# Preparing the two graphs of a pair side by side, with the edge test on VectorE and the counts of other entries on ScalarE

## The chip, the cores and the metric

The kernel runs on one core of one Trainium2 chip. The metric is the device time of one execution in microseconds (us). The core has five engines that run at the same time and each take their instructions in order: PE (TensorE, the matrix unit), DVE (VectorE), ACT (ScalarE), POOL (GpSimd) and SP (SyncE, which here only issues transfers). ACT and POOL issue transfers as well. An instruction that waits holds up everything behind it on its own engine.

## The reference

There are 16 graphs of 1024 nodes with 64 channels, given as `x` (16, 1024, 64), a symmetric float32 adjacency of zeros and ones `adj` (16, 1024, 1024) and a node mask. Each layer works on `h = relu(layernorm(x))`.

```
# layer 0, per graph
neigh = (adj > 0) & ~eye                     # the neighbours of each node
rank  = cumsum(neigh) - neigh;  nb = neigh.sum(-1)
skip  = ceil(nb / 2) if nb > 10 else 1
rem   = neigh & (skip > 1) & (rank % skip == skip - 1) & mask ;  rem |= rem.T
nd    = (neigh & ~rem) | eye                 # what stays: the "live" neighbours
agg   = .25*q25 + .5*q50 + .25*q75           # quantiles over live neighbours, per channel
x = x + MLP(h + agg) * mask
# layer 1: three graph convolutions  x_i = bn(relu(adj @ (x_{i-1} @ W_i) + b_i)), then a linear layer
```

## The kernel before

**Two stages.** The first stage finds the live neighbours and the quantiles for 8 pairs of graphs, one pair after another; the second (`later`) runs the dense part of both layers and is woven into the end of the first.

**Within a pair.** Preparing a pair (`prepare`) reads the adjacency in 8 tiles of 128 rows for each graph and ends with a table `r` that numbers every node's live neighbours. Nodes are sorted by their number of live neighbours and cut into eight blocks (`BLOCKS` and `TAIL`) of 200 to 16 columns. For each block `gather` builds selection masks on DVE (tile `s`, L987), multiplies them with the features on PE (tile `pg`, L1018; the two graphs fill the two halves of the partitions), and copies the sums out on ACT (tile `g`, L1023). `quantiles` then sorts the slots of the block with a network of min and max on DVE (L935), weighted with coefficients from ACT (L868, L871), and multiplied and added on DVE (L941, L950). The block that is sorted and the block that is gathered are one apart. Seven of the block steps of a pair also carry a share of the next pair's preparation.

**The preparation of one graph** (`prepare_one`, then `find_live` and `number_slots`, which it returns). For each of 8 row tiles: a 512 KB load into tile `a` (two buffers, L664, issued by SP), ACT makes `edge` by the sign (L671), DVE counts entries that are neither 0 nor 1 into `odd` (L673), PE transposes (`ptE`, L678), ACT copies the result into `edgeT` (L681). SP then sends `edgeT` to memory (L684) for the second stage, and DVE clears its diagonal (`own`, L686), so it waits for that transfer. Then come the row sums (`sums`, L651), the running counts (`cs` on PE, `stays` on ACT and DVE, L725 and L726), the live edges with their number `nv` (`q` on PE, L752 on ACT), and the place of each node in the order by degree: `key` (L758), eight comparisons on ACT (L770), `place` (L773). POOL sends the rows to memory by place (L778, eight indirect transfers) and fetches them again in order (`lp`, L794, two buffers); PE and ACT transpose them into `liveT` (L809, L812); sums, `nvs` (L822) and a test against `bounds` (L829, L833) follow; `number_slots` writes `r` in two sides of eight copies each (L851). `prepare` ends with the weights `z` (L615 to L618) and the three bf16 parts `hp` of the features (L625 to L628). Only when `r` side 0, `z` and `hp` of both graphs are there can the next pair's first block be gathered.

**What sets the order.** Everything is written as generators whose `yield`s are steps. `weave` draws them by share of the sort done; `SHARES` says how many preparation steps each block carries, 93 in a pair. Before, the two graphs follow each other: all of `prepare_one` for graph 0 and then for graph 1, then `find_live` and side 0 of `number_slots` for each. Side 1 of both is kept for the next pair's first steps. From this order a planner makes the final order of every engine's queue at build time: it may let an instruction pass earlier ones on its engine, but on the chip each queue then runs strictly in order. Buffers by name: `a` has two, `byte` (for `edge`, `edgeT`, `liveT`) four, `stays` one, the PSUM tile `big` two, `coef` one.

**The rest that the change touches.** `bounds` is a constant tile filled on POOL at the start (L472 to L492). At the end a flag is formed from `odd` and `beyond` (L1496 to L1509); if it is set, a general path runs, which this data never needs.

Of the kernel before, what the change touches and what calls it, by code (L numbers as in the profile page):

```python
# [10 lines left out]
F32 = mybir.dt.float32  # L11
# [19 lines left out]
SHARES = (10, 9, 17, 24, 20, 13, 0)  # L31
# [368 lines left out]

@with_exitstack
def graph_layers_kernel(ctx: ExitStack, tc: tile.TileContext, ins, out: bass.AP):
# [61 lines left out]
    bounds = const.tile([C, HALF], BF16, name="bounds")  # L464
# [7 lines left out]
    with tc.tile_pool(name="setup", bufs=2) as setup:  # L472
        for c in range(1, NT + 1):
            most, least = [(-float(N), 0, N)], [(0.0, 0, N)]
            for (j0, j1, few, slots), (first, end, fewer) in zip(BLOCKS + (TAIL,), NEAR):
                if c == NT:
                    least.append((float(few), j0, j1))
                    most.append((-float(slots), j0, j1))
                    for k in sorted(fewer, reverse=True):
                        most.append((-float(k), j0, j0 + fewer[k]))  # L480
                if c in first:
                    most.append((-float(first[c]), j0, j1))
                if c in end:
                    least.append((float(end[c]), j0, j1))
            for row, pieces in ((c - 1, most), (NT + c - 1, least)):
                line = setup.tile([1, N], BF16, tag="line", name="line")
                for value, a, b in pieces:
                    nc.gpsimd.memset(line[:, a:b], value)
                for hf in range(NH):
                    nc.gpsimd.dma_start(  # L490
                        out=bounds[32 * hf + row : 32 * hf + row + 1, :], in_=line[:, hf * HALF : (hf + 1) * HALF]
                    )  # L492

    odd = const.tile([P, NB, NT], F32, name="odd")
# [74 lines left out]

    h_d = [dram.tile([N, C], F32, name=f"h_d{b}") for b in range(NB)]  # L570
# [14 lines left out]
    def prepare(p, pools):  # L585


        work, keep, ps = pools
        st = Pair()
        st.p = p  # L590
# [14 lines left out]
        find_live, number_slots = [], []  # L605
        for x in range(2):
            find_live.append((yield from prepare_one(st, x, pools)))
        for x in range(2):
            number_slots.append((yield from find_live[x]()))
            yield from number_slots[x](0)  # L610
# [19 lines left out]
        st.number = itertools.chain(*(number_slots[x](1) for x in range(2)))  # L630
# [23 lines left out]
    def prepare_one(st, x, pools):  # L654
# [14 lines left out]
        for t in range(NT):  # L669
            a, coming = coming, load(t + 1) if t + 1 < NT else None  # L670
            nc.scalar.activation(edge[:, t, :], a, AF.Sign, saturate=False)  # L671
            junk = work.tile([P, N], F8, tag="junk_v", name="junk_v")
            nc.vector.scalar_tensor_tensor(  # L673
                junk, a, 1.0, a, ALU.is_equal, ALU.not_equal, accum_out=odd[:, b, t : t + 1], saturate=False
            )
            pt = ps.tile([P, NT, P], F32, tag="big", bufs=2, name="ptE")
            for u in range(NT):
                nc.tensor.matmul(  # L678
                    out=pt[:, u, :], lhsT=edge[:, t, u * P : (u + 1) * P], rhs=ident_h, start=True, stop=True
                )  # L680
            nc.scalar.activation(edgeT[:, :, t * P : (t + 1) * P], pt, AF.Copy, saturate=False)  # L681
            yield
# [105 lines left out]
        def find_live():  # L788
# [36 lines left out]
            for hf in range(NH):  # L825
                sl = slice(hf * HALF, (hf + 1) * HALF)
                rows = slice(32 * hf, 32 * hf + 2 * NT)
                nc.tensor.matmul(out=by[:, sl], lhsT=chunk_to, rhs=sums[:, sl], start=True, stop=False)
                nc.tensor.matmul(  # L829
                    out=by[:, sl], lhsT=ident_h[rows, rows], rhs=bounds[rows, :], start=False, stop=True  # L830
                )
# [588 lines left out]
    with ExitStack() as stack:  # L1420
# [7 lines left out]
        with ExitStack() as inner:  # L1428
# [3 lines left out]
            )  # L1432
            ahead = Steps(prepare(0, early))
# [60 lines left out]
    with ExitStack() as stack:  # L1494
        ps = stack.enter_context(tc.tile_pool(name="ps_flag", bufs=1, space=PSUM))
        most_odd = const.tile([P, 1], F32, name="most_odd")  # L1496
        nc.vector.tensor_reduce(most_odd, odd.rearrange("p b t -> p (b t)"), AX.X, ALU.max)
        worst = const.tile([P, 1], F32, name="worst")
        nc.vector.tensor_copy(worst, most_odd)
        most_beyond = const.tile([2 * NT, 1], F32, name="most_beyond")  # L1500
        nc.vector.tensor_reduce(most_beyond, beyond, AX.X, ALU.max)
        nc.vector.tensor_tensor(worst[: 2 * NT], worst[: 2 * NT], most_beyond, ALU.max)
        pd = ps.tile([1, P], F32, name="pd")
        nc.tensor.transpose(pd, worst, ident)
        most = const.tile([1, 1], F32, name="most")
        nc.vector.tensor_reduce(most, pd, AX.X, ALU.max)
        nc.vector.tensor_scalar(most, most, 0.0, None, ALU.is_gt)
        flag = const.tile([1, 1], I32, name="flag")
        nc.vector.tensor_copy(flag, most)  # L1509
# [28 lines left out]
```

## Time and profile before

| what | value |
|---|---|
| median of 3 runs (lowest, highest) | 3160.63 us (3157.54, 3173.24) |
| the profiled execution | 3163.56 us, of it span 3161.8 us |
| PE busy | 2599.2 us (82% of the span) |
| DVE busy | 2559.8 us (81%) |
| ACT busy | 1696.2 us (54%) |
| POOL busy | 619.5 us (20%) |
| mean granted clock of PE | 0.915 |
| until the first mask `s` of the first pair | 205.8 us |
| from the first mask of one pair to that of the next | 299.4, 300.1, 300.2, 293.0, 351.5, 294.1, 300.4 us |
| from the last pair's first mask to the end | 817 us |

The busy times are averages over stages of different kinds, so they are read by stage. The fifth interval between pairs is longer because the tails of four pairs are sorted in it. The times of first masks are starts of the first 128x3200 instruction of L987 in each pair, taken from the order of instructions in time (205.80, 505.23, 805.29, 1105.45, 1398.46, 1749.98, 2044.03, 2344.39 us).

### The profile page before, as it was taken

To read this page: it belongs to the slowest core of one execution; us is meant where nothing else is said; L and a number is where in the kernel's file an instruction comes from. 1 tells how busy PE (TensorE), PEld (TensorE's weight loads), DVE (VectorE), ACT (ScalarE), POOL (GpSimd) and SP (SyncE) were. 2 spreads that over 40 slices of the span, in tenths; PEclk is the share of its full clock that TensorE was granted. 3 is DMA by queue.
4 is the path that set the end of the run, shared out by engine and by line. 5 is a ranking of instruction groups with operands and counts; after the bars stand their busy time and mean duration, and the time that the engine had idled before them with its cause. 6 is when DMAs were issued, how large, how long until landed. Compare 5 with 4: busy or idle time off the path is not lost.

```text
span 3161.8 us, 67201 instructions
## 1 busy us (share of the span) xinstructions
PE 2599.2 (82%) x27849; PEld 1697.4 (54%) x27849; DVE 2559.8 (81%) x5895; ACT 1696.2 (54%) x3292; POOL 619.5 (20%) x545
## 2 busy tenths in 40 slices
PE   2678978898888889885798889888986688977778
PEld 1445655565556556653565566456643456644445
DVE  4149889998999799989998999899976979963332
ACT  4764666567557755774367557745853223332221
POOL 5110161022102200330022103300422530311110
PEclk9779999999899999997899999999987799988989
DMA  4131022111211212122111211211113011122211
GB/s 138 46 104 60 3 67 70 56 55 52 66 57 54 64 56 68 46 72 47 42 64 51 66 56 57 67 56 63 48 36 75 9 41 26 49 55 54 54 54 42
DMA packets 221082, 177.45 MB, mean 56 GB/s; under 512 B 189024, under 2 KB 189152, under 8 KB 216672
## 3 DMA queue, kind: packets, MB, share of 16 engines
q1 hardware_dynamic: 141824, 125.88, 13.1%
q0 software_dynamic: 17408, 37.81, 3.9%
q10 hardware_dynamic: 61536, 9.39, 1.7%
q8 instruction: 219, 3.59, 0.5%
q14 instruction: 95, 0.78, 0.1%
HBM read 124.44 MB, written 48.55 MB: 55 GB/s over the span
## 4 chain that ended last, share of the span: by engine, by line
DVE 40%; PE 29%; ACT 12%; DMA 8%; issue 6%; another core or an unknown queue 2%; POOL 2%; ACTq 1%; DVEq 0%; POOLq 0%; SPq 0%
PE pg L1018 11%; DVE t L935 10%; DVE s L987 9%; DVE g L935 8%; PE pg L1200 5%; ACT junk L770 3%; DMA a<-in_adj 3%; DMA lp<-live_d 3%; DVE junk_v L673 2%; PE pr L845 2%; DVE g_tails L935 1%; DVE t_tails L935 1%; PE keys L763 1%; PE pf L1216 1%
## 5 line engine op out<-in xcount | busy, mean ns | idle before, releaser
L1018 PE MATMUL pg<-s,hp 128*64 128x400 bf16 (+11 forms) x16848 | 1366.5, 313 | 172.3 <-DVE s L987 138.1
L1018 PEld LDWEIGHTS <-hp 128*64 128x64 bf16 x16848 | 894.5, 112 | 553.9 <-issue 109.6
L987 DVE TENSOR_SCALAR s<-r 128x3200 bf16<-128x3200 bf16 (+25 forms) x1312 | 623.6, 521 | 103.6 <-PE pg L1018 74.9
L778 POOL DMA_INDIRECT live_d<-edge,place x128 | 261.1, 2040 | 1354.3 <-DVE place L773 1149.9
L1023 ACT COPY g<-pg 128x400 f32<-128x400 f32 (+10 forms) x384 | 169.0, 443 | 399.4 <-PE pg L1018 363.1
L935 DVE TENSOR_TENSOR t<-g 128x600 f32<-128x600 f32 (+9 forms) x524 | 315.5, 626 | 34.0 <-ACT g L1023 33.2
L1200 PE MATMUL pg<-adjT,xw 128*64 128x512 fp8e4 x2304 | 284.5, 398 | 52.8 <-ACT xw L1185 25.7
L935 DVE TENSOR_TENSOR g<-t 128x96 f32<-128x96 f32 (+16 forms) x555 | 283.2, 537 | 1.2
L1243 POOL DMA_INDIRECT agg<-agg_d,place x128 | 171.2, 1338 | 495.2 <-PE pt L1131 258.2
L671 ACT ACTIVATE edge<-a 128x1024 fp8e4<-128x1024 f32 x128 | 135.1, 1058 | 214.4 <-DMA a<-in_adj 213.9
L1200 PEld LDWEIGHTS <-xw 128*64 128x64 bf16 x2304 | 140.1, 114 | 182.4 <-issue 42.0
L868 ACT ACTIVATE coef<-z,bias 128x200 f32<-128x200 bf16 (+6 forms) x480 | 173.9, 405 | 102.3 <-DVE agg L950 66.0
L935 DVE TENSOR_TENSOR t<-t 128x192 f32<-128x192 f32 (+20 forms) x447 | 207.8, 475 | 0.2
L871 ACT ACTIVATE coef<-coef,wcol 128x200 f32<-128x200 f32 (+7 forms) x512 | 189.6, 403 | 9.3 <-issue 7.1
L673 DVE SCALAR_TENSOR_TENSOR junk_v<-a 128x1024 fp8e4<-128x1024 f32 x128 | 155.4, 1214 | 24.4 <-DMA a<-in_adj 24.4
L845 PE MATMUL pr<-liveT,upto 128*128 128x512 fp8e4 (+2 forms) x384 | 127.4, 350 | 53.1 <-ACT r L851 46.9
L770 ACT ACTIVATE junk<-keys,minus 128x1024 fp8e4<-128x1024 f32 x128 | 144.3, 1128 | 38.1 <-PE keys L763 34.3
L851 ACT CAST r<-pr 128x592 bf16<-128x592 f32 (+1 forms) x256 | 142.5, 585 | 41.1 <-PE pr L847 32.1
L794 POOL DMA_DIRECT2D lp<-live_d x128 | 89.4, 699 | 376.9 <-PE pt L809 319.3
L812 ACT ACTIVATE liveT<-pt 128x1024 fp8e4<-128x1024 f32 x128 | 130.3, 1034 | 50.5 <-PE pt L809 47.1
L752 ACT ACTIVATE edge<-q,bias 128x1024 fp8e4<-128x1024 f32 x128 | 141.8, 1108 | 22.6 <-PE q L747 22.6
L725 ACT ACTIVATE stays<-cs,back 128x1024 f16<-128x1024 f32 x128 | 136.7, 1111 | 31.1 <-PE cs L721 15.9
(182 smaller groups left out, 3879.4 us busy)
## 6 DMA issues: line engine op xcount, KB each, us to landing
a<-in_adj SPq DMA_DIRECT2D x128, 512.0 KB
adjT_d<-edgeT SPq DMA_DIRECT2D x16, 1024.0 KB
lp<-live_d POOLq DMA_DIRECT2D x128, 128.0 KB
adjT<-adjT_d SPq DMA_DIRECT2D x16, 1024.0 KB
room<-in_x SPq DMA_DIRECT2D x16, 256.0 KB
h_d<-room SPq DMA_DIRECT2D x16, 256.0 KB
h_again<-h_d SPq DMA_DIRECT2D x16, 256.0 KB
xt<-in_x SPq DMA_DIRECT2D x16, 256.0 KB
```

Of the source, the lines that this page charges most:

```text
L673: nc.vector.scalar_tensor_tensor(junk, a, 1.0, a, ALU.is_equal, ALU.not_equal, accum_out=odd[:, b, t : t + 1], saturate=False)
L770: nc.scalar.activation(junk, keys, AF.Sign, bias=minus[:, t : t + 1], accum_out=above[:, t : t + 1], saturate=False)
L778: sent = nc.gpsimd.indirect_dma_start(out=live_d[b][:, :], out_offset=bass.IndirectOffsetOnAxis(ap=place[:, b, t : t + 1], axis=0), in_=ed ...
L845: nc.tensor.matmul(out=pr[:, o], lhsT=upto, rhs=liveT[:, u, sl], start=True, stop=(u == 0))
L868: nc.scalar.activation(coef[:, i, :], z[:, at], AF.Abs, bias=bias(rank - (slots + 1) // 2 + tau), scale=sign)
L871: nc.scalar.activation(coef[:, i, :], coef[:, i, :], AF.Relu, bias=wcol[:, q : q + 1], scale=-w)
L935: nc.vector.tensor_tensor(view(bufs, o, n1, n2), view(bufs, a, n1, n2), view(bufs, b, n1, n2), ALU.max if op else ALU.min)
L987: nc.vector.tensor_scalar(s[:, k, :, us, w0:], r[:, :, us, at + w0 : at + W], float(LIVE + 1 + k0 + k), None, ALU.is_equal)
L1018: summed = nc.tensor.matmul(out=pg[x * C : (x + 1) * C, ks, w0:], lhsT=st.hp[:, part, x, u, :], rhs=s[:, ks, x, u, w0:], start=(whole and ...
L1023: nc.scalar.copy(g[:, k0 : k0 + n, :], pg)
L1200: nc.tensor.matmul(out=pg[cs, :], lhsT=part[:, u, cs], rhs=adjT[x][:, u, sl], start=(u == 0 and k == 0), stop=(u == NT - 1 and k == len(xw ...
L1243: nc.gpsimd.indirect_dma_start(out=agg[:, t, x, :], out_offset=None, in_=agg_d[b][:, :], in_offset=bass.IndirectOffsetOnAxis(ap=place[:, b ...
```

## The change

It does four things.

- The edge tile is made on DVE by a comparison with 1 (a `tensor_scalar`); the DVE count `odd` goes. ACT makes two passes over `a` instead of one, both only for their accumulated sums: one of the signs, one of `relu(-2^100 * a)`. The copy of the transposed tile into `edgeT` accumulates as well (`ones`).
- The two graphs of a pair are drawn in turns: graph 0 goes 20 steps ahead, then one step each. A row tile counts as two steps. `SHARES` grows from 93 to 109 steps.
- `bounds` is filled in the pool of the preparation, with its work line in the ring of `sums`.
- The flag at the end is formed from the three counts.

```diff
-SHARES = (10, 9, 17, 24, 20, 13, 0)
+SHARES = (12, 11, 20, 28, 23, 15, 0)
+BEHIND = 20
+def in_turns(one, other):
+    while one.step():
+        yield
+        if other.step():
+            yield
@@ prepare
-        find_live, number_slots = [], []
-        for x in range(2):
-            find_live.append((yield from prepare_one(st, x, pools)))
-        for x in range(2):
-            number_slots.append((yield from find_live[x]()))
-            yield from number_slots[x](0)
+        one, other = (Steps(prepare_one(st, x, pools)) for x in range(2))
+        for _ in range(BEHIND):
+            one.step()
+            yield
+        yield from in_turns(one, other)
+        find_live = [Steps(one.result())]
+        yield from in_turns(find_live[0], other)
+        while other.step():
+            yield
+        number_slots = [find_live[0].result]
+        find_live.append(Steps(other.result()))
+        yield from in_turns(Steps(number_slots[0](0)), find_live[1])
+        while find_live[1].step():
+            yield
+        number_slots.append(find_live[1].result)
+        yield from number_slots[1](0)
...
-        st.number = itertools.chain(*(number_slots[x](1) for x in range(2)))
+        st.number = in_turns(*(Steps(number_slots[x](1)) for x in range(2)))
@@ prepare_one
             a, coming = coming, load(t + 1) if t + 1 < NT else None
-            nc.scalar.activation(edge[:, t, :], a, AF.Sign, saturate=False)
-            junk = work.tile([P, N], F8, tag="junk_v", name="junk_v")
-            nc.vector.scalar_tensor_tensor(
-                junk, a, 1.0, a, ALU.is_equal, ALU.not_equal, accum_out=odd[:, b, t : t + 1], saturate=False
-            )
+            nc.vector.tensor_scalar(edge[:, t, :], a, 1.0, None, ALU.is_equal, saturate=False)
+            for scale, func, count in ((1.0, AF.Sign, signs), (-float(2**100), AF.Relu, negative)):
+                junk = work.tile([P, N], F8, tag="junk", name="junk")
+                nc.scalar.activation(
+                    junk, a, func, scale=scale, accum_out=count[:, b, t : t + 1], saturate=False
+                )
             pt = ps.tile([P, NT, P], F32, tag="big", bufs=2, name="ptE")
...
-            nc.scalar.activation(edgeT[:, :, t * P : (t + 1) * P], pt, AF.Copy, saturate=False)
+            nc.scalar.activation(
+                edgeT[:, :, t * P : (t + 1) * P], pt, AF.Copy, accum_out=ones[:, b, t : t + 1], saturate=False
+            )
+            yield
             yield
```

## The prediction

> **What bounds the kernel now.** I read the page's busy shares, then the busy time by stretches, then the order in time around the joint between two pairs, then groups and waits. The two stretches below run from the first mask of a pair to its first `key`, and from the second `place` to the next pair's first mask (columns: us, then busy PE, PEld, DVE, ACT, POOL, clock, transfers):
>
> ```profile
> PE 2599.2 (82%) x27849; PEld 1697.4 (54%) x27849; DVE 2559.8 (81%) x5895; ACT 1696.2 (54%) x3292; POOL 619.5 (20%) x545
> ```
>
> ```profile
> 1105.45:1270.86 165.41, 143.71 (x1706) 94.50 (x1705) 164.43 (x302) 90.51 (x178) 3.38 (x3) 0.96 0.19 61
> 1347.41:1398.46 51.05, 45.24 (x503) 26.37 (x500) 40.28 (x152) 38.71 (x82) 17.71 (x17) 0.93 0.27 77
> ```
>
> For 165 us after a pair begins DVE is never idle: it is the bound there, and what it is relieved of is gained, what it waits for is lost. At the joint it idles (40.3 busy of 51.1): a chain over POOL, PE and ACT from the second `place` to a finished `r` sets the pace, and DVE's other work only covers it. The dense stage after 2780 us is PE's and is not touched.
>
> ```profile
> 109.09 0.17 DVE L773 TENSOR_SCALAR place<-above 128x8 int32<-128x8 f32 x1 [17.87 <-ACT junk L770]
> ...
> 161.33 0.17 DVE L773 TENSOR_SCALAR place<-above 128x8 int32<-128x8 f32 x1 [12.62 <-ACT junk L770]
> ...
> 205.80 1.89 DVE L987 TENSOR_SCALAR s<-r 128x3200 bf16<-128x3200 bf16 x2
> ...
> 1048.91 0.16 DVE L773 TENSOR_SCALAR place<-above 128x8 int32<-128x8 f32 x1
> ```
>
> From the second `place` to the first mask the first pair, where nothing else is on PE, takes 44.5 us (161.33 to 205.80). At the seven joints it takes 58.7, 58.4, 56.5, 51.1, 59.4, 51.5, 58.8, mean 56.3 (for instance 1048.91 to 1105.45).
>
> ```profile
> L673 DVE SCALAR_TENSOR_TENSOR junk_v<-a 128x1024 fp8e4<-128x1024 f32 x128 | 155.4, 1214 | 24.4 <-DMA a<-in_adj 24.4
> ...
> L616 DVE TENSOR_SCALAR half<-half 128x1024 f32<-128x1024 f32 x8 | 5.5, 688 | 0.1
> ...
> L671 ACT ACTIVATE edge<-a 128x1024 fp8e4<-128x1024 f32 x128 | 135.1, 1058 | 214.4 <-DMA a<-in_adj 213.9
> ...
> L770 ACT ACTIVATE junk<-keys,minus 128x1024 fp8e4<-128x1024 f32 x128 | 144.3, 1128 | 38.1 <-PE keys L763 34.3
> ```
>
> ```profile
> ACT edge L671 <- DMA a<-in_adj: 213.9, 88, 6.6
> ```
>
> These give prices and a warning: ACT waited 88 times, 2.4 us each, for a load. ACT has room for that. DVE hardly waits for loads (24.4 us, nearly all before the first pair), since its count stands late in its queue.
>
> **The change, part by part.**
>
> *DVE's tile work.* Out go 128 counts of 1.21 us and 128 accumulator reads of 0.08 (they follow each other at 1.22). In come 128 comparisons of one source, float32 to fp8. No row has that form. Bounds: 0.69 (the same form writing float32) and 1.21 (the count, which writes fp8). I take 0.69, as the nearest in form, 0.61 from start to start: 0.61 less per tile, 9.8 us per pair, 68 us over the seven pairs that follow the first. Were it 1.21, the gain would be about 1 us per pair.
>
> The Trainium skill's page "VectorE: DVE Perf Modes" (the perf-mode tier table) says that a float32 `tensor_scalar` in SBUF runs at two elements per cycle and a two-tensor operation at one; the rows 688 and 1214 agree. Its companion "Vector Engine (DVE) Microarchitecture Reference" (5.1) asks nothing of the output's type for that mode; no row here shows it for fp8, and it would mean 0.69. The page "ScalarE: Activation LUTs" (Rules for kernel authors) speaks against the change: simple functions belong on VectorE. By it the counts would stay on DVE and the 68 us would not be there.
>
> *ACT.* Per tile one pass (0.97 from start to start) goes, two with a sum come (1.1 each, from L770, which stands at 1.10 to 1.26), and the copy to `edgeT` gets a read (about 0.13): 1.4 more, 23 per pair. ACT goes from 188 to 211 us of 300. It stays below DVE, so this costs only through what stands behind it.
>
> *The load ring.* This is where I expect the loss. A buffer of `a` came free after one ACT pass and DVE's count; now after DVE's comparison and both passes. The comparison is needed at once (PE's transposes wait for it), and the order of the changed kernel shows it early in DVE's queue: the eight of graph 0 stand around the change from one pair's sort to the next, with 1 to 4 instructions between them. So the wait for loads moves from ACT to DVE. Around the joint, by hand (a load at 4.3 us, as on the chain of waits, where most take 4.3 to 4.9; coefficients 0.36 each): the sum `negative` of the third tile stands in ACT's queue behind the block's 18 coefficients, which need the previous sort's end. From the first mask, that end comes at 13 us, the coefficients and three copies take it to 21, `negative` ends at 22.3. The fourth copy `g` is behind it, at 22.7, and the first comparators of the new sort need it: DVE has only 17.5 us of work until there, so it idles 5. The fifth tile's load goes out at 22.3 and lands at 26.5; DVE gets there at 24.2, another 2; smaller ones 1. Sum 8 per pair. In graph 1 the 12th to 15th comparisons stand 0.7 to 3 us apart while the ring gives a tile every 3.5: about 5 per pair. Bounds for both together: 0 (all landed in time) and 36 (2.4 for each of 15). I take 13, or 91 in seven.
>
> *The joint.* In turns, graph 1's `place` comes at step 86 of 109; before it was 58 of 93. In DVE's queue only 82 small comparators (96 to 192 wide), 14 small masks and about eight 1024-wide operations then stand between it and the next pair's first mask; before 69 larger comparators and 68 masks. Priced at 0.06 us plus 1.05 ns per float32 element (600 elements 0.70) and 0.06 plus 0.27 ns for masks (3200 elements 0.91) that is 25.5 against 37.8. The work is not gone; it lies ahead of `place`. The chain: PE is freer, since the small gathers are done by then, and POOL's eight sends no longer stand between the last fetches of graph 0. Bounds: 44.5 (undisturbed) and 56.3 (the mean now). I take 48, nearer the undisturbed one. Idle 22.5 against 18.5: plus 4 per pair (0.5 to 12.3), plus 28 in seven.
>
> *The first pair.* Nothing covers it; it is pure chain. Graph 0: ACT spends 3.3 per tile where 2.9 was the loads' pace, and the seven `edgeT` copies of graph 1 stand among graph 0's `nv` and comparisons: its `place` at about 116.5 instead of 109.1. Graph 1: the sums of its 14th to 16th tiles stand behind all eight comparisons, so load 16 goes out only at 119, its `edgeT` copy stands behind two `liveT` copies, which need `place`, eight sends (1.27 each), and a fetch: 136 instead of about 109. Then SP's store of `edgeT` (5.2, as before) and `own`: 142 instead of 114.7. From there `place` comes about 47 later (46.6 before), at 190 instead of 161.3, the first mask 44.5 later: 234 instead of 205.8. Plus 28 (10, if graph 0's delay alone counts, to 35).
>
> *At nothing:* filling `bounds` (POOL's 30 us of setup, over before `sums` need the ring), the flag (six small operations under the dense stage), and POOL's and SP's further transfers, whose number does not change. SP's store of graph 0 now stands behind 14 loads, but `own` behind 15 us of DVE's sort; without that cover up to 5 per pair.
>
> *Sum,* against the profiled execution: 3163.6 + 28 - 68 + 91 + 28 = 3243. It lies 2.9 over the median, so the forecast is 3240.
>
> **The rivals.**
> *A, faster: DVE's relief decides.* If loads land before the comparisons (ring 0) and the joint costs 0.5, the sum is 3160.6 + 28 - 68 + 4 = 3125. For it: DVE's 100% stretch, and that almost no instruction on DVE waits now. Against: ACT's 88 waits for the same loads. It decides once ring and joint together cost under 5.5 us per pair.
> *B, no change:* ring and joint at 5 to 7 cancel the relief and half of the first pair's delay: 3160.
> *C, the first pair alone:* ring and joint cancel DVE's gain: 3188.
> *D, the comparison does not run fast:* 1.21 instead of 0.69 takes 60 back: 3300. Against: the 688 row.
> *E, ACT becomes the bound:* if half of its added 186 us reaches the copies `g` that PE and DVE wait for, 93 more, 3330. Against: 70% of a pair.
>
> **How the numbers follow.** The forecast's own case (3200 to 3280) 0.50; A 0.13; B 0.10; C 0.12; D and E together 0.15. About 0.5% (16 us) is what a measurement can tell from no change. Faster is A: 0.13; same is B: 0.10; slower is the rest: 0.77. The range 3150 to 3310 leaves out most of A and the end of E.
>
> **What would show it.** In the changed kernel's profile: the comparison near 0.69; waits of DVE for `a`, 70 us or more after the first pair, in place of ACT's; the first mask near 234; from the last `place` to the next first mask 45 to 51, DVE idle in over 20 of it; intervals between first masks near 307 instead of 300. I am wrong if the comparison seldom waits for its load, or if the first mask comes near 206.

## The result

The changed kernel takes 3430 us (median of 4 runs, 3425 to 3440) against 3162 us for the kernel before on the same chip: 1.0836 times as long, 95% interval 1.0813 to 1.0859, some 265 us. The forecast was 3240 us with a range to 3310: the direction was right, the size was far too small.

The profiled execution spans 3438.5 us, 276.7 more than before. The first masks of the eight pairs divide that up. The first one comes at 236.70 (205.80 before, +30.9); from the first to the eighth it takes 2378.7 us (2138.6 before, +240.1); from the eighth to the end 823.1 (817.4 before, +5.7). So most of it, 240 of 277 us, is lost in the seven pairs that are prepared beside another pair's sort: 330.5 to 333.8 from mask to mask where 300 was usual and about 307 was forecast (385.8 and 351.5 for the pair with the long sort).

### The profile page after: what moved, and what is told of

It reads as the page before. It is cut to its first block, busy times and chain, and to the rows that moved or that the text cites. A ratio compares the mean times of both kernels' runs of the same rounds, so it can differ in the third digit from the quotient of the medians.

```text
span 3438.5 us, 67595 instructions
## 1 busy us (share of the span) xinstructions
PE 2616.8 (76%) x27827; PEld 1735.1 (50%) x27850; DVE 2503.9 (73%) x5770; ACT 1858.8 (54%) x3804; POOL 552.1 (16%) x545
## 4 chain that ended last, share of the span: by engine, by line
issue 47%; DVE 16%; PE 14%; ACT 7%; DMA 6%; POOL 5%; another core or an unknown queue 3%; ACTq 0%; POOLq 0%; DVEq 0%; SPq 0%
PE pg L1230 4%; DMA lp<-live_d 4%; DVE t L965 4%; DVE g L965 4%; DVE s L1017 3%; POOL agg L1273 3%; PE pg L1048 2%; ACT junk L800 2%; POOL live_d L808 1%; DMA live_d<-edge,place 1%; PE pt L839 1%; PE pf L1246 1%; PE py L1185 1%; PE pm L1181 1%
## 5 line engine op out<-in xcount | busy, mean ns | idle before, releaser
L1048 PEld LDWEIGHTS <-hp 128*64 128x64 bf16 x16848 | 923.9, 115 | 561.0 <-DVE s L1017 131.0
L808 POOL DMA_INDIRECT live_d<-edge,place x128 | 242.3, 1893 | 1897.8 <-DVE place L803 1664.5
L699 ACT ACTIVATE junk<-a 128x1024 fp8e4<-128x1024 f32 x256 | 270.7, 1058 | 119.0 <-DMA a<-in_adj 115.5
L839 PE MATMUL pt<-ident_h,lp 128*128 128x128 bf16 x1024 | 101.1, 261 | 265.5 <-DMA lp<-live_d 263.9
L965 DVE TENSOR_TENSOR g<-t 128x96 f32<-128x96 f32 (+15 forms) x555 | 284.1, 540 | 1.7
L1273 POOL DMA_INDIRECT agg<-agg_d,place x128 | 179.1, 1399 | 510.5 <-PE pt L1161 203.9
L839 PEld LDWEIGHTS <-lp 128*128 128x128 fp8e4 x1024 | 78.4, 118 | 285.7 <-DMA lp<-live_d 279.1
```

Source lines behind the costliest of these rows:

```text
L699: nc.scalar.activation(junk, a, func, scale=scale, accum_out=count[:, b, t : t + 1], saturate=False)
L808: sent = nc.gpsimd.indirect_dma_start(out=live_d[b][:, :], out_offset=bass.IndirectOffsetOnAxis(ap=place[:, b, t : t + 1], axis=0), in_=ed ...
L839: nc.tensor.matmul(out=pt[:, u, :], lhsT=lp[:, u * P : (u + 1) * P], rhs=ident_h, start=True, stop=True)
L965: nc.vector.tensor_tensor(view(bufs, o, n1, n2), view(bufs, a, n1, n2), view(bufs, b, n1, n2), ALU.max if op else ALU.min)
L1048: summed = nc.tensor.matmul(out=pg[x * C : (x + 1) * C, ks, w0:], lhsT=st.hp[:, part, x, u, :], rhs=s[:, ks, x, u, w0:], start=(whole and ...
L1273: nc.gpsimd.indirect_dma_start(out=agg[:, t, x, :], out_offset=None, in_=agg_d[b][:, :], in_offset=bass.IndirectOffsetOnAxis(ap=place[:, b ...
```

## The profile after

The page of the changed kernel, busy shares and the chain that ended last:

```profile
PE 2616.8 (76%) x27827; PEld 1735.1 (50%) x27850; DVE 2503.9 (73%) x5770; ACT 1858.8 (54%) x3804; POOL 552.1 (16%) x545
...
issue 47%; DVE 16%; PE 14%; ACT 7%; DMA 6%; POOL 5%; another core or an unknown queue 3%; ACTq 0%; POOLq 0%; DVEq 0%; SPq 0%
```

DVE has 56 us less to do, as it was meant to, and ACT 163 more. No engine has become the bound: the largest share fell from 82% to 76%, and ACT's stands at 54% as before. When no engine is near full and the time grows, engines wait for each other, and the question is in which stretch.

One pair by stretches, first the kernel before, from 805.30, then the changed one, from 567.18. The five rows are: first mask to the first `key`, to the first `place`, to the second `key`, to the second `place`, to the next pair's first mask. Columns: length, busy PE, PEld, DVE, ACT, POOL, granted clock, busy share of the DMA engines, GB/s.

```profile
805.30:970.50 165.20, 143.85 (x1706) 94.59 (x1705) 164.39 (x302) 90.75 (x178) 8.66 (x3) 0.96 0.19 61
970.50:986.90 16.40, 15.96 (x179) 12.59 (x181) 15.33 (x24) 14.02 (x30) 0.00 (x0) 0.90 0.04 9
986.90:1032.00 45.10, 39.51 (x457) 26.13 (x457) 43.35 (x101) 32.75 (x60) 21.40 (x10) 0.96 0.17 58
1032.00:1049.00 17.00, 15.97 (x201) 12.10 (x203) 16.96 (x47) 14.73 (x25) 4.25 (x6) 1.00 0.23 61
1049.00:1105.50 56.50, 47.95 (x504) 25.70 (x500) 40.32 (x152) 38.70 (x82) 15.24 (x17) 0.88 0.23 67
```

```profile
567.18:741.49 174.31, 158.82 (x1926) 107.79 (x1925) 164.44 (x248) 109.92 (x234) 0.00 (x0) 0.98 0.16 52
741.49:757.72 16.23, 12.64 (x172) 9.59 (x173) 16.02 (x36) 14.29 (x28) 0.00 (x0) 0.91 0.02 5
757.72:838.64 80.92, 52.36 (x551) 33.41 (x547) 52.08 (x159) 45.61 (x89) 29.19 (x16) 0.79 0.16 50
838.64:853.41 14.77, 13.23 (x150) 10.33 (x152) 14.53 (x54) 12.47 (x25) 0.00 (x0) 1.00 0.14 30
853.41:898.96 45.55, 27.38 (x244) 16.27 (x246) 26.67 (x109) 28.97 (x61) 14.58 (x19) 0.70 0.28 85
```

The third row is the loss: 80.9 us in place of 45.1. DVE works 52.1 of them and stands still for 28.8, where it stood still for 1.8 before. The first row has grown by 9, nearly all of it idle DVE (9.9 in place of 0.8). The last row, the joint, has shrunk by 11, but DVE's idle time there hardly changed (18.9 and 16.2). Over the pair DVE works 6.6 us less and idles 38.2 more, and that is the 31.6 by which this pair is longer than the one before.

What DVE waits for in the changed kernel over the whole run (columns: us in total, times, longest), and PE's wait for the fetched rows; below them the same two waits, of `own` and of `pt`, in the kernel before:

```profile
DVE edgeT L716 <- DMA adjT_d<-edgeT: 162.0, 9, 25.3
...
DVE t L965 <- ACT g L1053: 93.1, 18, 9.8
...
DVE edge L695 <- DMA a<-in_adj: 59.4, 44, 5.8
...
PE pt L839 <- DMA lp<-live_d: 263.9, 58, 23.7
```

```profile
DVE edgeT L686 <- DMA adjT_d<-edgeT: 7.3, 3, 5.5
...
PE pt L809 <- DMA lp<-live_d: 41.5, 25, 9.3
```

L716 is `own`, which clears the diagonal of `edgeT` and must wait until SP's store of it has been read out. The timeline of the changed kernel around one such wait, engine by engine (start, length, what; in brackets the idle time just before it):

```profile
774.95 0.40 DVE L965 TENSOR_TENSOR g<-g,t 128x240 f32<-128x240 f32 x1
800.63 1.23 DVE L716 TENSOR_TENSOR edgeT<-edgeT,other_h 128x1024 fp8e4<-128x1024 fp8e4 x1 [25.28 <-DMA adjT_d<-edgeT]
...
758.17 18.09 POOL L808 DMA_INDIRECT live_d<-edge,place  x1 [195.37 <-DVE place L803]
776.56 0.99 POOL L808 DMA_INDIRECT live_d<-edge,place  x1 [0.30 <-issue]
...
784.17 0.96 POOL L808 DMA_INDIRECT live_d<-edge,place  x1 [0.30 <-DMA live_d<-edge,place]
787.13 1.15 POOL L824 DMA_DIRECT2D lp<-live_d  x2 [2.00 <-DMA live_d<-edge,place]
...
766.32 0.34 PE L1048 MATMUL pg<-s,hp 128*64 128x360 bf16 x1 [1.00 <-DVE s L1017]
789.49 1.89 PE L839 MATMUL pt<-ident_h,lp 128*128 128x128 bf16 x16 [22.83 <-DMA lp<-live_d]
...
792.61 0.62 PE L704 MATMUL ptE<-ident_h,edge 128*128 128x128 bf16 x8
...
790.55 1.94 ACT L842 ACTIVATE liveT<-pt 128x1024 fp8e4<-128x1024 f32 x2 [23.64 <-PE pt L839]
793.26 1.02 ACT L707 ACTIVATE edgeT<-ptE 128x1024 fp8e4<-128x1024 f32 x1 [0.77 <-PE ptE L704]
...
794.40 0.33 SPq L714 DMA_DIRECT2D adjT_d<-edgeT  x1
```

Read it backwards from 800.63. `own` of graph 1 waits for the store, issued at 794.40. The store waits for the copy of graph 1's last tile (793.26), which stands in ACT's queue behind two `liveT` copies of graph 0; that tile's transposes (792.61) stand in PE's queue behind two `pt` groups of graph 0. These wait for `lp`, which POOL fetches at 787.13 after eight sends. The tile's comparison on DVE had been done since 764.5. So graph 1's finished tile sits behind graph 0's round trip through memory, and DVE, with the sort behind `own` in its queue, sits behind the tile. On top of that the first send lasted 18.09 us. It ended at 776.26, 0.91 after DVE's last instruction (774.95 + 0.40): the sends made no headway until DVE had nothing left to do. The idle time is then a sum of links: 0.91, the other seven sends 8.87, landing and fetch 4.36, transposes and copies 4.91, store and `own` 6.23, together 25.28.

## The experiments

All ratios are to the kernel before on the same chip. "First mask" and "eight masks" (from the first to the eighth) are read in each profile; before they are 205.8 and 2138.6, in the changed kernel 236.7 and 2378.7. The rows stand on different chips, on which the kernel before took from 3128 to 3174 us. So two rows are compared by their ratios (a point is 1% of the time before, some 32 us); a difference of 20 to 30 us between two numbers in the last column can be the chips' alone.

| kernel | ratio, 95% interval | first mask | eight masks |
|---|---|---|---|
| changed | 1.0836, 1.0813 to 1.0859 | 236.7 | 2378.7 |
| order_alone | 1.0854, 1.0823 to 1.0886 | 228.6 | 2372.0 |
| ops_alone | 1.0246, 1.0228 to 1.0265 | 229.8 | 2168.1 |
| tiles_first | 1.0861, 1.0841 to 1.0880 | 233.4 | 2368.2 |
| pause | 1.0540, 1.0522 to 1.0558 | 236.3 | 2279.6 |
| pause_tiles | 1.0482, 1.0448 to 1.0516 | 233.0 | 2242.6 |
| fetch_last | 1.0248, 1.0227 to 1.0268 | 223.9 | 2180.3 |
| fetch_last_no_counts | 1.0007, 0.9988 to 1.0027 | 192.5 | 2148.2 |
| no_counts | 1.0793, 1.0767 to 1.0819 | 219.0 | 2361.8 |
| seq_no_counts | 1.0010, 0.9994 to 1.0026 | 195.0 | 2124.6 |
| seq_one_count | 1.0277, 1.0259 to 1.0296 | 218.6 | 2188.5 |
| before_no_count | 1.0035, 1.0020 to 1.0049 | 205.1 | 2141.5 |
| before_pause | 1.0074, 1.0046 to 1.0101 | 206.6 | 2147.0 |
| before_no_count_pause | 1.0047, 1.0025 to 1.0068 | 203.6 | 2162.7 |
| before_sp | 1.0313, 1.0287 to 1.0338 | 205.5 | 2249.0 |
| before_no_count_sp | 1.0250, 1.0219 to 1.0281 | 202.2 | 2218.9 |
| fetch_last_sp | 1.0538, 1.0505 to 1.0571 | 224.9 | 2301.3 |
| after_sp | 1.0674, 1.0641 to 1.0707 | 234.1 | 2344.1 |

### The order or the operations

`ops_alone` keeps the comparison, the counts and the sums, and takes back the order:

```diff
-SHARES = (12, 11, 20, 28, 23, 15, 0)
+SHARES = (10, 9, 17, 24, 20, 13, 0)
...
-        yield from in_turns(one, other)
-        find_live = [Steps(one.result())]
-        yield from in_turns(find_live[0], other)
...
+        for x in range(2):
+            find_live.append((yield from prepare_one(st, x, pools)))
+        for x in range(2):
+            number_slots.append((yield from find_live[x]()))
+            yield from number_slots[x](0)
```

> The changed kernel with the order of before: graph 0 of a pair through to its `place`, then graph 1, then both fetches; one step per tile and the old 93 steps with their old shares. Comparison on VectorE, both counts and the sum of ones on ScalarE stay. Theory O (the order: graph 1's last `edgeT` copy stands behind graph 0's fetch in PE's and ACT's queues, and VectorE's `own` waits for it): the wait of `own` is gone, first masks are 290 to 303 us apart (300 of before, minus 9.8 for the comparison, plus 0 to 13 for loads), total 3100 to 3190. Theory P (the added ScalarE passes and the later release of the load buffers cost it): total 3350 or more, first masks 325 or more apart.

`order_alone` does the opposite:

```diff
-            nc.vector.tensor_scalar(edge[:, t, :], a, 1.0, None, ALU.is_equal, saturate=False)
-            for scale, func, count in ((1.0, AF.Sign, signs), (-float(2**100), AF.Relu, negative)):
...
+            nc.scalar.activation(edge[:, t, :], a, AF.Sign, saturate=False)
+            nc.vector.scalar_tensor_tensor(
+                junk, a, 1.0, a, ALU.is_equal, ALU.not_equal, accum_out=odd[:, b, t : t + 1], saturate=False
+            )
```

> The changed order (side by side, 109 steps) with the tile work of before: Sign on ScalarE, the count on VectorE, no counts on ScalarE. Theory O: from the first `place` of a pair to the second `key` again near 80 us, of which VectorE idles 25 or more before `own`; total 3380 to 3480. Theory P: total 3150 to 3230, that stretch near 45 to 55.

The order alone loses 8.5%, as much as the whole change; from first `place` to second `key` takes 75 to 81 us in it, with 23 to 25 us before `own` in six of the seven pairs (in the other a mask waits 20 us for PE instead). The operations alone lose 2.5%, 24 us of it in the first pair (mask at 229.8) and some 4 to 6 us in each other pair; their total, 3221, is above the 3100 to 3190 that theory O gave. So theory O holds for the large part, and the operations cost something of their own, which neither theory had sized. The two losses do not add up in the changed kernel (8.4% and not 11). That what else is late costs nothing where DVE stands still for 28 us anyway would explain it; no run shows this by itself.

### Which link of the stall

`tiles_first` lets graph 1 finish its tile loop before graph 0's fetch begins:

```diff
+AHEAD = 5
...
         yield from in_turns(one, other)
+        for _ in range(AHEAD):
+            other.step()
+            yield
         find_live = [Steps(one.result())]
```

> The changed kernel, where graph 1 takes five more steps by itself (its last tile, the store, `own`) before graph 0's fetch begins. Theory O: the wait before `own` falls from 25 us a pair to under 8, the stretch from first `place` to second `key` from 80 to 52 to 60, total 3250 to 3310. If the fetch then holds up graph 1's `cs` in PE's queue instead, the wait is found there and the total stays at 3350 to 3430. Theory P: no change, 3420 to 3440.

Its second case came true: the total did not move, although `own` no longer waits. In the waits of this kernel between 758 and 846 (PE) and 758 and 832 (DVE) the same stall is one step on:

```profile
PE pt L843 <- DMA lp<-live_d: 14.6, 2, 13.6
...
DVE stays L760 <- ACT stays L759: 15.3, 2, 15.1
```

Now graph 1's `cs` and `stays` stand behind graph 0's `pt`. The first send is longer still, 19.8 us, since DVE has a little more work before it stops.

`pause` leaves the order alone and makes DVE stop early, for one microsecond:

```diff
             rows_sent.append(sent)
+            if t == 0:
+                passed = work.tile([P, 1], F32, tag="passed", name="passed")
+                cleared = nc.gpsimd.memset(passed, 0.0)
...
+                nc.vector.tensor_copy(seen, passed)
```

> The changed kernel with one addition: POOL clears a word behind the first of a graph's eight sends, and VectorE copies that word one to four instructions after `place`, so VectorE stands still until POOL is past the first send. Theory L (in the changed kernel the first send of graph 0 takes 18 us because VectorE runs without a break, and ends 0.9 us after VectorE stops): the first send takes 1 to 2.5 us, VectorE waits about 1 us at the copy, `own` waits 8 to 12 us instead of 25, total 3310 to 3350. If the 18 us are POOL's own: VectorE stands 17 us at the copy, and the total stays within 20 of 3430. Theory P: no change.

Timeline of `pause`, POOL and DVE after a first `place` at 745.69:

```profile
746.14 1.54 POOL L808 DMA_INDIRECT live_d<-edge,place  x1 [197.15 <-DVE place L803]
...
747.99 1.42 POOL L808 DMA_INDIRECT live_d<-edge,place  x1 [0.19 <-issue]
...
747.83 0.15 DVE L826 COPY seen<-passed 128x1 f32<-128x1 f32 x1 [1.04 <-POOL passed L819]
...
774.44 1.23 DVE L716 TENSOR_TENSOR edgeT<-edgeT,other_h 128x1024 fp8e4<-128x1024 fp8e4 x1 [9.82 <-DMA adjT_d<-edgeT]
```

A stop of 1.04 us shortens the send from 18.1 to 1.5 and the wait of `own` from 25.3 to 9.8; the ratio falls by 3.0 points, some 93 us. That settles theory L: the 18 us are neither POOL's work nor the transfer's, but DVE's unbroken run.

`pause_tiles` has both edits.

> The changed kernel with both edits at once: VectorE stands still for the first send, and graph 1 takes five steps by itself before graph 0's fetch begins. Theory L with theory O (one stall of 28 us a pair, made of a send of 18 us held up and a fetch queued ahead of graph 1's work; each edit alone leaves the other part): first `place` to second `key` 52 to 58 us, no wait of `own` or of `stays` over 5 us, total 3210 to 3260. If the fetch is still ahead of `cs`: waits at `stays` of 8 us or more a pair, total 3290 to 3330.

The stretch came to 57 to 59 us with DVE busy for 55.9 of 58.5, and in the seven pairs after the first `own` waits 0.6 us at most and `stays` 2.7 us in all. The time, 3282, is 22 above the range: the stall is gone, but the first pair (233.0) and the other stretches still lose; which of them was not separated.

`fetch_last` moves the cause itself and keeps everything else in turns:

```diff
-        find_live = [Steps(one.result())]
-        yield from in_turns(find_live[0], other)
         while other.step():
             yield
+        find_live = [Steps(one.result())]
+        while find_live[0].step():
+            yield
```

> The changed kernel, with graph 0's fetch (all its transposes `pt` and copies `liveT`) begun only when graph 1 has sent its rows, as in the order of before; the tile loops, `stays` and `nv` stay in turns. Theory O: no wait of `own` or of `stays` over 3 us a pair although the first send of graph 0 still takes 9 us or more, because nothing waits for it; first `place` to second `key` 50 to 58 us; the joint grows to what it was before (56 to 60); total 3230 to 3310. If the stall belonged to the turns themselves and not to the fetch: first `place` to second `key` stays at 75 or more, total over 3400.

Its pair from 524.3, the stretch from first `place` to second `key`, and the first send in it:

```profile
717.00:762.10 45.10, 40.49 (x440) 26.41 (x436) 37.63 (x101) 32.34 (x68) 27.68 (x10) 0.89 0.20 70
...
717.41 19.07 POOL L809 DMA_INDIRECT live_d<-edge,place  x1 [185.72 <-DVE place L804]
```

The stretch is back at 45 us, as before the change, although the send is held up for 19 us. Nothing waits for it there. From 1.0836 to 1.0248: of the 8.4 points 5.9 go with the place of graph 0's fetch in the queues. (Of DVE's 7.5 idle us in this stretch 5.2 are a wait for gather matmuls. The joint stayed at 43 to 51, below the 56 to 60 expected, and the total, 3209, came out below the range.)

### The counts on ACT

`no_counts` is the changed kernel without this loop, with the sums of ones left in:

```diff
-            for scale, func, count in ((1.0, AF.Sign, signs), (-float(2**100), AF.Relu, negative)):
-                junk = work.tile([P, N], F8, tag="junk", name="junk")
-                nc.scalar.activation(
-                    junk, a, func, scale=scale, accum_out=count[:, b, t : t + 1], saturate=False
-                )
```

> The changed kernel without its two counting passes on ScalarE (the check that no entry differs from 0 and 1 is left out; order and comparison stay). Theory O (the stall between first `place` and second `key` sets the loss, and it does not depend on the counts): `own` still waits 22 to 27 us a pair; only what VectorE waits behind the counts (2.3 us at the comparison and up to 10 us at the difference that needs a copy `g`, in a pair of 332) can go: total 3340 to 3420. Theory P (the passes): total 3150 to 3230.

It takes 271 us of passes off ACT and wins 0.4 points, some 14 us. The first mask alone comes 17.7 us earlier, so the seven other pairs win nothing. The wait of `own` is still there:

```profile
DVE edgeT L711 <- DMA adjT_d<-edgeT: 193.9, 9, 25.4
```

`seq_no_counts` is `ops_alone` without the loop, `fetch_last_no_counts` is `fetch_last` without it.

> The order of before with the comparison on VectorE and without the two counts (the check that no entry differs from 0 and 1 is left out). Against the same kernel with the counts (ratio 1.0246 to before, first mask at 229.8, pairs near 302 apart). If the counting passes hold the loads and the copies `g`: first mask 200 to 212, pairs near 290 (300 less 9.8), total 3060 to 3110. If the loads are held by where the comparison stands in VectorE's queue: first mask still 222 or later, pairs 295 or more, total 3150 to 3210.

> The changed kernel with graph 0's fetch after graph 1's `place` and without the two counts (that check is left out). If the loss of the change is a sum of two parts, the fetch's place in the queues (1.084 to 1.025) and the counting passes (in the order of before 1.025 to 1.001): ratio 0.997 to 1.006, first mask 200 to 208. If the counts cost nothing in turns (as in the changed kernel, where they were worth 0.4%): ratio 1.018 to 1.025.

In both orders the counts are worth the same: 1.0246 to 1.0010, and 1.0248 to 1.0007. In the first pair they cost 35 and 31 us, and by the ratios some 40 and 45 in the rest. With this the loss is accounted for: the fetch's place and the counts together are all of it, and what is left (comparison on DVE in place of Sign on ACT, graphs in turns) cannot be told from no change. How it divides depends on which goes first: 5.9 points for the fetch and then 2.4 for the counts, or 0.4 for the counts (`no_counts`) and then 7.9 for the fetch. But `seq_no_counts` was expected at 3060 to 3110, with pairs near 290, and came out at 3138, most pairs near 300. DVE's relief is missing.

`seq_one_count` sums once instead of twice:

```diff
+            nc.scalar.activation(
+                junk, a.bitcast(U32), AF.Sign, accum_out=signs[:, b, t : t + 1], saturate=False
+            )
```

> The order of before, comparison on VectorE, and one counting pass in place of two: ScalarE sums the Sign of the entries read as unsigned integers (any entry other than 0 counts once, the sum of ones is taken from it). The whole computation is kept. Bounds from the two kernels beside it: with no count ratio 1.001 and first mask 195.0, with two counts 1.0246 and 229.8. If each pass costs alike: ratio 1.010 to 1.016, first mask 208 to 216. If the second pass is what takes ScalarE's time per tile over the loads' pace: ratio 0.999 to 1.008, first mask 195 to 205.

Neither came true. One pass loses as much as two (1.0277 against 1.0246): less in the first pair (218.6 against 229.8), so more in the rest. So the loss is not in proportion to ACT's time. That the buffer `a` is read by a second engine late in its queue would fit, but no run shows it; this stays open.

### Where DVE's relief went

`before_no_count` is the kernel before with the count on DVE (L673) and the test of `odd` taken out:

> The kernel before without its count on VectorE (the check that no entry differs from 0 and 1 is left out; Sign on ScalarE and the order stay). It takes 1.22 us per tile, 19.5 per pair, off VectorE. If VectorE is the bound of the first 165 us of a pair, as it was forecast from its 100% share there: the eight counts in that stretch alone are 9.8 us a pair, total 3040 to 3070, stretch from first mask to first `key` near 155. If PE's chain stands right behind VectorE (seq_no_counts took half as much off VectorE and won nothing): total 3100 to 3130, the stretch stays over 160 and VectorE idles in it.

19.5 us per pair less on DVE, and the time is 0.35% longer: the second case, but for the total (3158), which is above both. In the kernel before all sixteen counts of a pair stand between its neighbour's first mask and its own first `key` (the expectation took eight), so 137 us were taken out of the seven such stretches. Only some 32 were won there (155 to 164 us each instead of 164 to 166, the pair with the long sort aside); from the second `key` to `half` 37 came back. Two waits of DVE in all, at `key` for ACT's `edge` and at the masks for the gather matmuls, first before and then without the count:

```profile
DVE s L987 <- PE pg L1018: 74.9, 46, 10.3
...
DVE key L758 <- ACT edge L752: 30.0, 3, 11.6
```

```profile
DVE s L983 <- PE pg L1014: 159.7, 59, 15.3
...
DVE key L754 <- ACT edge L748: 64.7, 9, 11.6
```

What DVE gained, it waited longer for PE and ACT. Within the seven stretches to the first `key` its waits rose by 70 us: 35 at `key` (some 6 in every pair, where before only one pair had any), 24 at masks, 17 for copies `g`. So the row in which DVE was never idle ran close beside a chain over PE and ACT of nearly the same length. Two explanations were open for the rest: held-up sends (in this kernel the sends of graph 0 took 44 us in most pairs, and the last two fetches of graph 0 stood behind graph 1's sends), or that chain itself. The fetches were moved to SP's queue in four kernels:

```diff
-                load = nc.gpsimd.dma_start(out=lp, in_=live_d[b][t * P : (t + 1) * P, :])
+                load = nc.sync.dma_start(out=lp, in_=live_d[b][t * P : (t + 1) * P, :])
```

> The kernel before with the sixteen fetches of a pair issued by SyncE instead of POOL; nothing else changes. In the kernel before graph 0's fetches were rarely behind a held send (pt waited 2.7 us for lp in a pair): 0 to 1% faster, ratio 0.990 to 1.000. If SyncE's queue, where a fetch that waits holds the next pair's loads, costs more than it saves: 1.002 to 1.015.

> The kernel before without its count on VectorE (that check is left out) and with the fetches issued by SyncE. Theory Q (what VectorE was relieved of came back as held sends with graph 0's fetches behind them in POOL's queue): the wait of `pt` for `lp`, 20.6 us in a pair without this edit, falls under 5, and the ratio is 0.96 to 0.985. Theory R (PE's chain bounds the pair as soon as VectorE does not): ratio 0.993 to 1.003 as without it.

> The changed kernel with graph 0's fetch after graph 1's `place`, fetches issued by SyncE. Without the latter the ratio is 1.0248. Theory Q: 1.005 to 1.018, since sends and fetches of the two graphs no longer share POOL's queue. Theory R: 1.020 to 1.030.

> The changed kernel with the fetches issued by SyncE; the order of the steps stays. Graph 1's last store and graph 0's first fetch now stand in one queue, the fetch first. Theory O with the held send: `own` still waits 20 us or more a pair, ratio 1.075 to 1.090, because the first send is held as before and the transposes stand in PE's queue as before. If POOL's issue of the fetch were part of the wait: 1.05 to 1.07.

That did not decide it, for it made the very stall of this case, now in the kernel before (1.0313, above both its cases). SP's queue and DVE in `before_sp`:

```profile
729.35 0.80 SPq L794 DMA_DIRECT2D lp<-live_d  x2
730.25 0.37 SPq L684 DMA_DIRECT2D adjT_d<-edgeT  x1
...
734.66 1.23 DVE L686 TENSOR_TENSOR edgeT<-edgeT,other_h 128x1024 fp8e4<-128x1024 fp8e4 x1 [15.27 <-DMA adjT_d<-edgeT]
```

The planner put graph 1's store behind graph 0's first two fetches, which wait for the sends, and `own` waits for the store: 43 to 45 us from first `place` to second `key` became 59 to 63, and the kernel lost 3.1%. The same stall stands in `before_no_count_sp` and `fetch_last_sp` (`own` waits 16 us in each of the seven pairs, first `place` to second `key` is 61 to 63), so their 1.0250 and 1.0538, above all that was expected of them, say nothing on theories Q and R. The changed kernel won 1.6 points by the same edit, as its second case had it, but its wait of `own` stayed (165 us in all); the joint became some 3 us shorter per pair.

The sends were then freed by the pause instead, in the kernel before and in the one without the count.

> The kernel before with the pause alone. Its first send of graph 0 also takes 9 to 20 us, but the fetch that needs it begins only after graph 1's `place`. Theory O: that time is hidden; the first send falls to 1 to 2 us, and the total is the same or up to 0.5% longer (VectorE stands about 1 us, 14 times). If a held-up send cost time by itself: 60 to 90 us faster.

> The kernel before without its count on VectorE (that check is left out) and with VectorE standing still for the first send of each graph. Theory Q (the relief is lost to held-up sends in POOL's queue, with fetches behind them): the sends of graph 0 are over 12 to 14 us after they begin instead of 44, ratio 0.965 to 0.990. Theory R (PE's chain bounds the pair): ratio 0.998 to 1.010, and VectorE waits for PE's `pg` at the joint as long as without the pause (28 us in a pair).

In `before_pause` the first send of graph 0 takes 1.0 to 1.9 us in the seven pairs, where it took 11.9 to 19.9, and the time rises by 0.7%: what nothing waits for is worth nothing, and the pause costs a little (more than the 0.5% expected). In `before_no_count_pause` graph 0's sends take 12 us instead of 44, and the relief is still not there (1.0047); DVE waits 165.6 us for `pg`. Even with the pause's own 0.7 points taken off, 0.3 points are won of the 4.3 that 19.5 us per pair would be. So held-up sends do not explain where the relief went. What is left is the chain over PE and ACT: that it bounds the pair is inferred from the waits above, and which link of it is the last was not separated.

No kernel that computes everything came out faster than the one before.

## Why the prediction was wrong, point by point

- **The first pair, +28: right.** Mask at 236.7 (234 forecast). The links came as worked out: `place` 117.2 (116.5), last load out at 119.6 (119), store at 136.5 (136), `own` at 140.7 (142), second `place` at 190.6 (190).
- **"At nothing: ... SP's store of graph 0 ... `own` behind 15 us of DVE's sort; without that cover up to 5 per pair": this is the step that failed.** It looked at graph 0's store. Graph 1's is the late one, by the very chain that was worked out for the first pair and not asked for again in the seven others. There DVE does have work to cover it, 17 us, but the cover held the sends up: graph 0's eight, priced at 1.27 each, took 25 to 27 us in place of 10, with graph 1's last tile behind them and the fetch. So `own` waited 184 us in the whole run (162.0 for the store by the list, and 22.4 that the list puts down to ACT), 18.6 in the first pair and 22 to 25 in each of the others. First `place` to second `key`, 43 to 45 us before, became 77 to 81; with the fetch moved (`fetch_last`) it is 44 to 47 again and 5.9 of the 8.4 points are gone. None of the rivals had this; E came nearest in microseconds, by a mechanism that `no_counts` refutes.
- **"what it is relieved of is gained", -68: wrong.** The price was right: 128 comparisons took 0.69 us each, and DVE's busy time fell by 56 of the 78 that this price gives for eight pairs; where the rest stayed was not followed. (The 0.69 agrees with the Trainium skill's page "Vector Engine (DVE) Microarchitecture Reference", 5.1, whose conditions for two results per cycle in SBUF do not ask for a type of the output. The rule of "ScalarE: Activation LUTs", "Rules for kernel authors", puts `relu` and other simple functions on VectorE; the two counts on ACT cost 0.4 to 2.4 points here.) The value was zero: `seq_no_counts` and `before_no_count` took 9.8 and 19.5 us per pair off DVE and won nothing (1.0010 and 1.0035). A row in which DVE is never idle shows that DVE is busy there, not that the pair would end earlier.
- **The load ring, +91: mis-sized.** In the pair shown the copy `g` held the sort up for 2.8 us (5 forecast), the comparisons waited for loads for 2.0 us near the pair's beginning (2 and 1 forecast) and 0.3 in graph 1 (5 forecast): 5.1 in place of 13. Over the seven stretches from first mask to first `key` the waits are 26.7 for loads and 23.0 for `g`, 7 per pair. But a wait is not its worth: without the counts the waits for `g` in the seven pairs fall from 89 to 16 us, those of `half` for ACT's `nvs` rise from 29 to 72, and the seven pairs are no faster. By the runs, what the counts delay is worth nothing in the changed kernel's seven pairs, and some 40 to 45 where the stall is absent. The first pair pays 18 to 35 more, which the forecast had in its first term.
- **The joint, +28: right in its parts.** 45 to 47 us from the second `place` to the mask (48 taken), DVE busy for 26.7 of them (25.5), idle 18.9 (22.5) in the pair shown. Before it idled 15.5 on average and not 18.5, so the seven joints gained 24 us of idle time (28 forecast).
- **ACT at 211 us of a pair: right** (211.25 in the pair shown), and it is not the bound.
- **Intervals near 307: wrong,** 330 to 334.

The comparison seldom waited for its load: 26.7 us after the first mask, where 70 or more were forecast. The prediction itself had named that as a sign that it was wrong. Two readings of it were off as well, without weight in the sum: of the 24.4 us that DVE waited for loads before, a third (8.0) lay behind the first mask; and rival B's 5 to 7 us per pair (35 to 49) come to no change only with the whole of the first pair's 28 beside them, not half.

## What to carry to other kernels

When two chains are put in turns, look at each in-order queue for the first instruction of one chain that waits for a round trip through memory, and list what of the other chain is behind it; then ask where that one's consumer stands. A chain worked out for a stretch without cover has to be asked for again in the covered stretches, since cover can also be what holds it up. And before a relief is booked at its full length, take the work away altogether and see whether the time moves: here 19.5 us per pair off the busiest engine of a stretch moved nothing.

## What the hardware showed

An indirect send on POOL, 1.0 us when DVE stands still, can be held up for as long as DVE runs without a break. In the changed kernel the first send of graph 0 lasted 16.4 to 18.1 us in each of the seven pairs and ended 0.9 after DVE's last instruction. In the kernel before the same thing stands in the trace (minimum, median and maximum of this line are 956, 1168 and 19941 ns) and could have been read there. One such send of it, and DVE's instructions around its end at 700.87:

```profile
687.33 13.54 POOL L778 DMA_INDIRECT live_d<-edge,place  x1 [167.25 <-DVE place L773]
...
699.09 0.88 DVE L935 TENSOR_TENSOR t<-g 128x704 f32<-128x704 f32 x1
700.00 1.58 DVE L935 TENSOR_TENSOR g<-t 128x528 f32<-128x528 f32 x3
```

DVE's instructions normally overlap by about 0.08 us. Between 699.97 and 700.00 there is a gap of 0.03, and the send ends 0.90 after its beginning. Of the 141 sends over 4 us in these nineteen kernels, 106 end 0.8 to 1.2 after such a gap or after DVE's stop, and none has a gap earlier inside it: a break of a few hundredths of a microsecond is enough. The other 35 ended without one; in eight of them, the 19.94 among them, DVE's short copy `nb` out of PSUM stands 0.8 to 1.0 before the end. The Trainium skill's page "SBUF — State Buffer" ("Who interferes with whom") says that VectorE and GpSimd share a pair of SBUF ports under an exclusive lock, and that a transfer issued by GpSimd waits for it because GpSimd writes its descriptors. The held sends and `pause` agree with that. One thing differs: the page's probe did not see two-input operations hold such transfers up, but between 690.22 and 694.80, inside the send shown, DVE ran nothing else, and the send did not end. And one stays open: in the kernel before, the later sends of a graph took 1.0 to 2.4 us each, but for two (3.0 and 11.9), while DVE was just as busy; why mostly the first one is held is not shown.
